# A conditioned feed-forward block: side 0 of the first pair turned by VectorE and transfers, output tiles, conditioning and weight sums in another order, a seed in an accumulator apart

## The chip, the core and the metric

The kernel runs on one NeuronCore of a Trainium2 chip. The metric is the device time of one execution in microseconds (us). The engines are TensorE (PE in the profile; its weight loads are PEld), VectorE (DVE), ScalarE (ACT), GpSimd (POOL) and SyncE (SP). SP computes nothing here: it issues transfers. Each engine runs its own queue strictly in the order in which the kernel writes it down, and waits for other engines by semaphores.

## The reference

Inputs are x of 32 sequences x 128 tokens x 512 channels, one condition vector of 512 per sequence, and a mask of the tokens (true only for the padding at the end of a sequence, so for few of them). In short:

```python
m = mask[:, :, None]
emb = silu(t) @ ada_w + ada_b                      # per sequence: shift, scale, gate
norm = where(m, layernorm(x) * (1 + scale) + shift, 0)
fwd = gelu(norm @ ssm_w1 + ssm_b1) @ ssm_w2 + ssm_b2      # bwd the same with its weights
x = x + gate_msa * where(m, fwd + bwd, 0)          # changes masked tokens only
shift_mlp, scale_mlp, gate_mlp = split(silu(t) @ ffada_w + ffada_b, 3)
ff_norm = layernorm(x) * (1 + scale_mlp) + shift_mlp
h = gelu_tanh(ff_norm @ ff_w1 + ff_b1)             # 512 -> 1024
out = x + gate_mlp * (h @ ff_w2 + ff_b2)           # 1024 -> 512
```

All is float32.

## The kernel before, in words

**Opening.** The first half changes masked tokens only, so the kernel collects them in 512 slots, four tiles of 128. For the first pair only slots 0 to 255 (tiles 0 and 1) matter. `hidden` (L184) makes the hidden layer of two tiles, `project` (L198) the second product into `po_s`, and `finish_slots` adds bias, multiplies by the gate, adds x (L200, L201, L289, on DVE) and stores the tile to `x1_rows` in DRAM (L290, SP). `take_first_half` (L652, POOL) then gathers the changed rows from there into the tiles of x; `Statistics` (L684 to L690; the root runs on POOL) and `normalised` (L696) make the normalised x.

Beside that the opening prepares the second half:

- `combine_weights` makes sums of the quarters of a weight matrix (four instructions of DVE), for `fw1` and later for `fw2`.
- `weight_sums(1)` to `weight_sums(4)` (L570, DVE) make further sums of `fw1` and store them to `t_rows` in DRAM (L572 to L575, SP), from where `load_weights` reads them as `tw`. Sums 1 and 4 use two tiles `spare` (named x), sums 2 the tile `t_2`, sums 3 a tile `tw_3` of its own.
- The conditioning of the second half: `pm_f` (L254, PE) is the product with `ffada_w`, `mod2` (L264, DVE) the result with its bias. It is transposed on PE into `ptr_mod` (L616) and copied to `modT`, from which the per-channel scale and shift come. Its gate rows go to `gate_rows` in DRAM (POOL).
- In the order of PE's queue: `po_s` of tile 0, `pm_f`, `po_s` of tile 1, the gate rows of tiles 2 and 3 (`part_s`, L274, which share three accumulators with `po_s` and `pm_f`), `ptr_mod`, then the hidden layer of tiles 2 and 3, and their `po_s`.

**The second half** takes the 32 sequences in four pairs of sides; a side is four sequences, so 512 tokens. Its input must lie with channels on the partitions (`xT`). In the first pair PE transposes the normalised tiles between the products of `po_s` (`transposed`, L705), and ACT (L714) and DVE (L710) in turn apply scale and shift. In the later pairs DVE turns blocks of 32 x 32 in place (STREAM_TRANSPOSE, L1225), 16 transfers per side put the blocks in place (`turned`, L725), and ACT scales them (`scaled`, L731).

`TokenBlocks` (L761, DVE) makes sums of the quarters of `xT` (s1, s2, a third that overwrites a quarter of side 1, and s4). The product with `ff_w1` is a scheme of seven products in place of eight, nested twice: seven products (numbers 1, 2, 5, 6, 3, 7, 4 in `STREAMS`), each made of seven phases P1 to P7. A phase (`FirstProduct.phase`, L879) is four passes on PE into one of two accumulators `e` and `a` of its product. P1, P6, P7 and P4 go to `a`, P5, P2 and P3 to `e`. After P5 `e` is copied away (`p_m`, L893); `seed` then puts `a` into `e` (L923 on DVE, L925 on ACT for product 1), and P2 adds to that. After P6 DVE writes `a` plus P5's result into `e` (L904), P3 adds to it; P7's and P4's results leave `a` through DVE (L909, L914). `window` interleaves the phases of a product with the last ones of the product before it, and puts smaller work, listed in `fills`, at places between them. `with_p5` (L930) and `late_sum` (L963) are sums on POOL.

The second product, with `fw2`, is one such scheme of 14 steps (`ORDER`, `SecondProduct.step`, L1059), into accumulators `a_o` and `e_o`; `first_block` (L1013) makes the sums that P5 takes. Between its first two steps stand the last phases of product 4, and `blocks(0, i)` for the next pair: normalise and turn sequence i of side 0.

The whole program is a `manual_schedule`: the order on each engine is that of the code.

Of the kernel before, what the change touches and what calls it, by code (L numbers as in the profile page):

```python
# [9 lines left out]
F32 = mybir.dt.float32  # L10
# [3 lines left out]
AF = mybir.ActivationFunctionType  # L14
# [8 lines left out]
def kernel(  # L23
# [49 lines left out]
    nc = tc.nc  # L73
# [217 lines left out]

    def combine_weights(w, rows, cols, t):

        b11, b12 = w[:, :rows, :cols], w[:, :rows, cols:]
        b21, b22 = w[:, rows:, :cols], w[:, rows:, cols:]
        t2, t3, t4 = (t[:, j] for j in range(3))
        nc.vector.tensor_tensor(t3, b22, b12, ALU.subtract)
        nc.vector.tensor_tensor(b12, b12, b11, ALU.subtract)
        nc.vector.tensor_tensor(t2, b22, b12, ALU.subtract)
        nc.vector.tensor_tensor(t4, b21, t2, ALU.subtract)  # L300
        return {"P1": b11, "P2": b21, "P3": b22, "P4": t4, "P5": b12, "P6": t2, "P7": t3}

# [242 lines left out]
    def in_blocks(t):  # L545
        return t.rearrange("p g (h f) -> p (g h) f", f=2 * P)
# [3 lines left out]
        2: [t_2.rearrange("p j k d -> p (j k) d")],  # L550
        4: [in_blocks(t) for t in spare],
    }

    def sum_block(j, n):
# [26 lines left out]
    for c in range(2):  # L581
        h1 += hidden(xT_s, NH, w1, 0, AF.Gelu, "s0", ssm, range(4 * c, 4 * c + 3))
        rows = slot_part(2 + c, 1, ps_o, "o"), slot_part(2 + c, 0, ps_o, "o")
        gs.append(keep_gate(c, slot_part(c, 2, ps_o, "o")))
        xn_s.append(modulated(xc[2 + c], *rows, f"s{2 + c}", xn[:, 2 + c]))
        if c == 0:
            combine_weights(fw1, KC // 2, FF // 2, t_1)
# [24 lines left out]
    gs = [keep_gate(c, slot_part(c, 2, ps_o, "o")) for c in (2, 3)]  # L612
# [87 lines left out]

    def transposed(g, xn, xT, k, by_vector):

        ptr = ps_t.tile([P, 512], F32, tag="tr", name=f"ptr_{g}_{k}")
        for i in range(G):
            nc.tensor.transpose(ptr[:, ts(i, P)], xn[i][:, ts(k, P)], ident)  # L705
        for i in range(G):
            b = g * G + i
            shift, scale = modT[:, k, b : b + 1], modT[:, k, B + b : B + b + 1]
            if by_vector:
                nc.vector.tensor_scalar(  # L710
                    xT[:, k, ts(i, P)], ptr[:, ts(i, P)], scale, shift, ALU.mult, ALU.add
                )
            else:
                nc.scalar.activation(  # L714
                    xT[:, k, ts(i, P)], ptr[:, ts(i, P)], AF.Identity, bias=shift, scale=scale
                )

# [81 lines left out]
    class FirstProduct:  # L799


        def __init__(self, p, x, w):
            self.p, self.x, self.w = p, x, w
            self.h = [
                hp.tile([P, HC, G * S], F32, tag=f"h{j}", name=f"h{j}_{p}") for j in "ab"
            ]
            self.banks, self.p5, self.tw = {}, {}, {}
            self.sx, self.held = {}, []

# [177 lines left out]
    class SecondProduct:  # L987
# [53 lines left out]
        def step(self, step):  # L1041
            p, ha, hb, s1, w = self.p, self.ha, self.hb, self.s1, fw2_of
            hh = HC // 2
# [72 lines left out]
    stats[1].one(0)  # L1116
    stats[1].one(1)

    def second_side():

        stats[1].one(2)
        stats[1].one(3)
        stats[1].root()
        for c in range(2):
            both = ssm.tile([P, 2, D], F32, tag="xT", name=f"xn_0_1_{c}", bufs=2)
            for i in range(2):
                xn_b.append(stats[1].normalised(2 * c + i, both[:, i]))

    xn_b = []

    def token_blocks(xT):
        of_x[0] = TokenBlocks(0, xT)
        for j in (1, 2, 3, 4):
            of_x[0].one(j)

    def turn(side, k):
        transposed(side, (xn_a, xn_b)[side], xT[side], k, by_vector=k % 2)

    def turns(*which):
        return lambda: [turn(side, k) for side, k in which]  # L1140

    finish_slots(
        2,
        h1,
        gs[0],
        {
            1: turns((0, 0)),
            2: turns((0, 1)),
            3: lambda: (second_side(), turn(0, 2)),
            4: turns((0, 3)),  # L1150
            6: turns((1, 0)),
            7: turns((1, 1)),
        },
    )
    finish_slots(3, h1, gs[1], {1: turns((1, 2)), 2: turns((1, 3)), 4: lambda: token_blocks(xT)})
    first_half.close()
# [15 lines left out]
    now.token_sums(2, 0)  # L1172
    now.do(1, "P7")
    now.with_p5(2, "22")
    now.token_sums(2, 1)
    now.do(2, "P2", "P6")
    now.token_sums(2, 2)
    now.token_sums(2, 3)
    now.do(1, "P4")
    for p in range(NP):  # L1180
        more_pairs = p + 1 < NP
# [24 lines left out]
        if more_pairs:  # L1206
            if p == 0:
                x_of[1] = load_x(1, spare)
            x_next = x_of[p + 1]
            stats = [Statistics(x_next[side], f"{p + 1}_{side}") for side in range(2)]  # L1210
            xn, xT = {}, {}

            def blocks(side, i):

                if i == 0:
                    t = (
                        group_of_tiles(f"{p + 1}_0")
                        if side == 0
                        else sp.tile([P, G, D], F32, tag="s12", name=f"xn_{p + 1}_1")
                    )  # L1220
                    xn[side] = t.rearrange("p i d -> p (i d)").rearrange(
                        "p (k i c) -> p k i c", i=G, c=P
                    )
                t = stats[side].normalised(i, xn[side][:, :, i])
                nc.vector.transpose(t, t)  # L1225
# [32 lines left out]
        fill = {5: [lambda: second.third_block(0)], 7: [lambda: second.third_block(1)]}  # L1258
        if more_pairs:

            def put(step, f, *args):
                fill.setdefault(step, []).append(lambda: f(*args))

# [159 lines left out]
```

## Time and profile before

| | before |
|---|---|
| median of 3 runs | 474.43 us (474.25 to 476.71) |
| the profiled execution | 474.88 us |
| its span, first to last instruction | 473.2 us |
| PE busy | 453.6 us, 96% |
| PEld busy | 367.9 us, 78% |
| DVE busy | 333.0 us, 70% |
| ACT busy | 175.5 us, 37% |
| POOL busy | 157.2 us, 33% |
| mean granted clock of PE | 0.996 |

Times in the profile count from the span's start. A line of a timeline has the start, the duration, the engine, the line of the kernel, the operation, the tiles written and read, the shape, and the number of instructions that are merged; in brackets the idle time of the engine ahead of it and what ended it. A line of the chain of waits has start, duration, what. A line of the windows view has the stretch, and for PE, PEld, DVE, ACT and POOL the busy time and number of instructions, then the granted clock, the share of the DMA engines that was busy, and GB/s. Rows of PE are overlapped: a pass of 256 columns is shown with 380 ns, but four in a row advance by 0.86 us.

### The profile page before, as it was taken

The page shows a single profiled execution, that of the slowest core. Times are in us where ns is not written, and L with a number is a line of the kernel's source. Part 1 is how long each engine was busy: PE and PEld are TensorE (multiplying, and loading weights), DVE is VectorE, ACT ScalarE, POOL GpSimd, SP SyncE. Part 2 cuts the span into 40 slices and gives each one's busy share as a digit, 9 for nine tenths or more (in the row PEclk, how much of TensorE's full clock was granted, in tenths as well). Part 3 has the DMA queues.
Part 4 walks back from the last instruction along what each step waited for, and adds up shares of the span by engine and source line. Part 5 has one row for each costly group of instructions (what it writes and reads, how often), then busy time and mean ns, then how long its engine had stood idle before and what let it go on. Part 6 is the DMA issues. An engine that isn't in the chain of part 4 may idle for free.

```text
span 473.2 us, 5833 instructions
## 1 busy us (share of the span) xinstructions
PE 453.6 (96%) x2016; PEld 367.9 (78%) x2016; DVE 333.0 (70%) x534; ACT 175.5 (37%) x380; POOL 157.2 (33%) x151
## 2 busy tenths in 40 slices
PE   6899997989999999999999999999999999999996
PEld 2374384458887888888878888888788888888885
DVE  4637686888778766997787488968875985433645
ACT  3122023325365074153643622545446134463000
POOL 6200035007975000189730002897200023760000
PEclk9999998999999999999999999999999999999999
DMA  8999930036314761844057428340773341303013
GB/s 277 386 408 355 403 151 14 23 130 242 110 57 118 150 89 46 320 166 160 3 175 125 100 75 280 129 159 3 215 104 82 123 167 33 124 34 145 0 61 120
DMA packets 73746, 69.35 MB, mean 147 GB/s; under 512 B 54689, under 2 KB 55217, under 8 KB 72691
## 3 DMA queue, kind: packets, MB, share of 16 engines
q1 hardware_dynamic: 63074, 57.42, 38.2%
q0 software_dynamic: 4256, 10.75, 6.7%
q10 hardware_dynamic: 6384, 0.79, 1.2%
q8 instruction: 17, 0.28, 0.2%
q14 instruction: 15, 0.11, 0.1%
HBM read 56.83 MB, written 13.17 MB: 148 GB/s over the span
## 4 chain that ended last, share of the span: by engine, by line
PE 56%; POOL 14%; DVE 11%; DMA 9%; issue 7%; ACT 1%; SPq 0%; POOLq 0%; DVEq 0%; ACTq 0%
PE a_o L1059 20%; PE e_o L1059 15%; PE a_m L879 9%; PE e_m L879 7%; POOL x L652 5%; DMA b2b<-in_L_cond_bwd_b_dram 4%; DVE xn L696 3%; POOL ha L930 2%; DMA t_rows<-x 2%; PE po_s L198 2%; DMA x<-x_rows,slot_i 2%; POOL ha L959 2%; POOL hb L959 2%; POOL hb L930 1%; DVE xn L1225 1%
## 5 line engine op out<-in xcount | busy, mean ns | idle before, releaser
L930 POOL TENSOR_TENSOR ha<-p_m,ha 128x512 f32<-128x512 f32 x20 | 27.7, 1387 | 172.8 <-ACT ha L937 163.6
L1059 PE MATMUL e_o<-fw,ha 128*128 128x256 f32 x256 | 57.9, 380 | 0.0
L1059 PE MATMUL a_o<-t,hb 128*128 128x256 f32 x240 | 54.1, 380 | 0.0
L1059 PEld LDWEIGHTS e_o<-fw,ha 128*128 128x128 f32 x256 | 48.8, 190 | 6.5
L1059 PEld LDWEIGHTS a_o<-t,hb 128*128 128x128 f32 x240 | 45.7, 190 | 6.1
L731 ACT ACTIVATE xT<-xT,modT 128x128 f32<-128x128 f32 x96 | 37.9, 479 | 25.9 <-DMA xT<-xn 25.8
L652 POOL DMA_INDIRECT x<-x_rows,slot_i x32 | 36.1, 1127 | 22.6 <-DMA x_rows<-t_s 13.9
L854 ACT ACTIVATE hb<-hb,biasT 128x256 f32<-128x256 f32 x64 | 29.0, 500 | 27.9 <-POOL hb L963 20.3
L893 ACT COPY p_m<-e_m 128x512 f32<-128x512 f32 x28 | 16.4, 586 | 60.1 <-PE e_m L879 60.1
L198 PE MATMUL po_s<-w,h_s 128*128 128x512 f32 x64 | 30.6, 614 | 0.0
L1059 PE MATMUL a_o<-t,s 128*128 128x256 f32 x128 | 28.9, 380 | 0.0
L1059 PE MATMUL a_o<-fw,ha 128*128 128x256 f32 x128 | 28.9, 380 | 0.0
L1059 PE MATMUL e_o<-fw,s 128*128 128x256 f32 x128 | 28.9, 380 | 0.0
L937 ACT COPY ha<-e_m 128x512 f32<-128x512 f32 x32 | 18.5, 579 | 27.7 <-PE e_m L879 23.8
L184 PE MATMUL ph_s<-xT_s,w 128*128 128x256 f32 x128 | 28.7, 383 | 0.0
L879 PE MATMUL a_m<-xT,tw 128*128 128x256 f32 x96 | 25.3, 386 | 3.5 <-DVE hb L909 3.5
L930 POOL TENSOR_TENSOR hb<-p_m,hb 128x512 f32<-128x512 f32 x20 | 28.2, 1411 | 0.3
L184 PEld LDWEIGHTS ph_s<-xT_s,w 128*128 128x128 f32 x128 | 24.0, 190 | 4.6 <-ACT h_s L188 1.5
L1059 PEld LDWEIGHTS a_o<-t,s 128*128 128x128 f32 x128 | 24.4, 190 | 3.2
L1059 PEld LDWEIGHTS a_o<-fw,ha 128*128 128x128 f32 x128 | 24.4, 190 | 3.2
L1059 PEld LDWEIGHTS e_o<-fw,s 128*128 128x128 f32 x128 | 24.4, 190 | 3.3
L684 DVE BATCH_NORM_STATS2 st<-x 128x6 f32<-128x512 f32 x32 | 21.9, 684 | 6.5 <-DMA x<-x_rows,slot_i 6.5
(194 smaller groups left out, 868.1 us busy)
## 6 DMA issues: line engine op xcount, KB each, us to landing
tw<-t_rows SPq DMA_DIRECT2D x16, 896.0 KB, 4.7
x<-in_x_dram SPq DMA_DIRECT2D x16, 512.0 KB, 6.9
gate<-gate_rows POOLq DMA_DIRECT2D x8, 1024.0 KB, 5.4
out_dram<-x SPq DMA_DIRECT2D x15, 512.0 KB, 3.3
xT<-xn SPq DMA_DIRECT2D x84, 64.0 KB, 2.8
fw<-in_L_cond_ff_w_dram SPq DMA_DIRECT2D x2, 2048.0 KB, 10.8
ada_f<-in_L_cond_ffada_w_dram SPq DMA_DIRECT2D x4, 768.0 KB, 16.0
ada_a<-in_L_cond_ada_w_dram SPq DMA_DIRECT2D x4, 512.0 KB, 6.2
```

Of the source, the lines that this page charges most:

```text
L184: nc.tensor.matmul(ph[:, :n], w[:, k, ts(f, P)], xT[:, k, :], start=(k == 0), stop=(k == KC - 1))
L198: nc.tensor.matmul(po, h[f][:, ts(i, P)], w[:, f, :], start=(f == 0), stop=(f == HC - 1))
L652: nc.gpsimd.indirect_dma_start(out=xs[i // G][i % G // 2][:, i % 2], out_offset=None, in_=x1_rows[:slots, :], in_offset=bass.IndirectOffse ...
L684: nc.vector.bn_stats(st, self.tile_at(i))
L731: nc.scalar.activation(xT[:, k, ts(i, P)], xT[:, k, ts(i, P)], AF.Identity, bias=modT[:, k, b : b + 1], scale=modT[:, k, B + b : B + b + 1],)
L854: nc.scalar.activation(dst[:, n], src[:, n], AF.Gelu_apprx_tanh, bias=biasT[:, f : f + 1])
L879: nc.tensor.matmul(bank[:, ts(n, QT)], self.w_block(j, product)[:, ts(n, P)], self.x_block(j, product), start=(product in ("P1", "P5") and ...
L893: nc.scalar.copy(p5, e)
L930: nc.gpsimd.tensor_tensor(self.place(RESULT[j], c), self.p5[j], other, ALU.add)
L937: nc.scalar.copy(self.place(RESULT[j], c), src)
L959: nc.gpsimd.tensor_tensor(part["12"], part["21"], other, ALU.add)
L1059: nc.tensor.matmul(part, src[:, k, ts(i, P)], w[product][:, k, :], start=(last and k == 0), stop=True, skip_group_check=True,)
```

## The change

1. `combine_weights` becomes a class, `Weights`, whose four sums can be made one at a time. For `fw2` they are no longer made together in the opening, but one each in windows 4 and 5 and in steps 2 and 6 of the second product of the first pair.
2. Weight sums 1 stand ahead of the sum of the biases; sums 3 and 4 directly behind slot tile 0, and slot tile 1 directly behind them. Sums 3 use the tiles of sums 1 again, sums 4 the tile `t_2` of sums 2. `mod2` comes after slot tile 1, on PE and on DVE. The store of `gate_rows` comes after the first six gathers.
3. Side 0 of the first pair is turned as in later pairs: by DVE and by 16 transfers, eight issued by SP and eight by ACT, then scaled on ACT. Side 1 is still transposed by PE, now only in slot tile 3 and behind it, and always scaled by DVE.
4. The first phases of products 1 and 2 come in another order, and product 1 has a third accumulator (`apart`): P5 goes into it, so that P1's result can be put into `e` before P5.
5. In every change of pair two of the four `blocks(0, i)` and the transfers come after phase P7 of product 4 instead of before P3, and the last statistic of side 1 comes later in window 6.

```diff
-    def combine_weights(w, rows, cols, t):
+    class Weights:
...
+            self.sums = [(t3, b22, b12), (b12, b12, b11), (t2, b22, b12), (t4, b21, t2)]
...
+        def combine(self, *which):
+            for j in which:
+                out, x, y = self.sums[j]
+                nc.vector.tensor_tensor(out, x, y, ALU.subtract)
...
         2: [t_2.rearrange("p j k d -> p (j k) d")],
-        4: [in_blocks(t) for t in spare],
     }
+    t_sum[3], t_sum[4] = t_sum[1], t_sum[2]
...
+    weight_sums(1)
     nc.vector.tensor_tensor(b2, b2, b2b, ALU.add)
     b2_row = dram.tile([1, D], F32, name="b2_row")
     nc.sync.dma_start(b2_row, b2[0:1, :])
-    weight_sums(1)
     weight_sums(2)
     finish_slots(0, h1, gs[0])
+    weight_sums(3)
+    weight_sums(4)
     transposed_slots(xn_s[1], xT_t[:, :, ts(1, P)], "s3")
+    finish_slots(1, h1, gs[1])
...
     modulation(pm, mod2, ada_f, modb_f, 0, 3)
-    gate_rows = dram.tile([B, D], F32, name="gate_rows")
-    nc.gpsimd.dma_start(gate_rows, mod2[2 * B : 3 * B, :])
...
-    t_sum[3] = [in_blocks(sp.tile([P, G, D], F32, tag="s12", name="tw_3"))]
-    weight_sums(3)
-    weight_sums(4)
-    finish_slots(1, h1, gs[1])
...
+        def apart(self, j):
+            e = ps_o.tile([P, 512], F32, tag="o", name=f"e_m{self.p}_{j}")
+            self.alone[j], a = accumulators(f"m{self.p}_{j}_alone")
+            self.banks[j] = e, a
+            self.p5[j] = None
...
             e, a = self.banks[j]
+            if product == "P5":
+                e = self.alone.pop(j, e)
...
     take_first_half(0, x_of[0], range(G + 2))
+    gate_rows = dram.tile([B, D], F32, name="gate_rows")
+    nc.gpsimd.dma_start(gate_rows, mod2[2 * B : 3 * B, :])
     h1 = hidden(xT_t, NH, w1, 0, AF.Gelu, "s1", ssm)
...
-    fw2_of = combine_weights(fw2, HC // 2, D // 2, t_2)
+    fw2_of = Weights(fw2, HC // 2, D // 2, t_2)
...
-    xn = group_of_tiles("0_0")
-    xn_a = [stats[0].normalised(i, xn[:, i]) for i in range(G)]
...
+    xn = in_turned_blocks(group_of_tiles("0_0"))
+    for i in range(G):
+        t = stats[0].normalised(i, xn[:, :, i])
+        nc.vector.transpose(t, t)
+    turned(xn, xT[0], (nc.sync, nc.scalar))
...
+    for k in range(KC):
+        scaled(0, xT[0], k)
...
-    finish_slots(3, h1, gs[1], {1: turns((1, 2)), 2: turns((1, 3)), 4: lambda: token_blocks(xT)})
+    finish_slots(2, h1, gs[0])
+    finish_slots(3, h1, gs[1], {4: lambda: turn(0), 6: lambda: turn(1)})
+    turn(2)
+    turn(3)
+    of_x[0] = TokenBlocks(0, xT)
+    for j in (1, 2, 3):
+        of_x[0].one(j)
...
+    now.apart(1)
     now.do(1, "P1")
+    now.seed(1)
     now.do(2, "P1")
+    now.do(1, "P2", "P5", "P6")
+    of_x[0].one(4)
+    now.do(2, "P5")
+    now.do(1, "P7")
+    now.with_p5(2, "22")
+    now.seed(2)
+    now.do(1, "P3")
+    now.with_p5(2, "12")
     for n in range(4):
         now.token_sums(1, n)
-    now.do(1, "P5")
-    now.seed(1)
-    now.do(2, "P5")
-    now.do(1, "P2", "P6", "P3")
-    now.seed(2)
-    now.with_p5(2, "12")
...
-    now.do(1, "P7")
-    now.with_p5(2, "22")
...
+                put(4, 1, fw2_of.combine, 0)
+                put(5, 1, fw2_of.combine, 1)
...
-            for i, at in enumerate(((4, 4), (4, 6), (5, 3), (6, 1))):
+            for i, at in enumerate(((4, 4), (4, 6), (5, 3), (6, 4))):
                 put(*at, stats[1].one, i)
...
         if more_pairs:
-            for i in range(G):
+            for i in range(2):
                 blocks(0, i)
-            to_feature_rows(0, nc.sync)
         now.do(4, "P3")
         second.seed(1)
         now.do(4, "P7")
+        if more_pairs:
+            for i in range(2, G):
+                blocks(0, i)
+            to_feature_rows(0, nc.sync)
         second.step(1)
...
+            put(2, fw2_of.combine, 2)
+            put(6, fw2_of.combine, 3)
```

More of the change, by code (lines that the diff above doesn't have):

```diff
@@ L290, in finish_slots, with __init__ @@
         nc.sync.dma_start(x1_rows[ts(at, P), :], t)
-    def combine_weights(w, rows, cols, t):
[L294 to L301, printed above, removed]
+    class Weights:
+        def __init__(self, w, rows, cols, t):
+            b11, b12 = w[:, :rows, :cols], w[:, :rows, cols:]
+            b21, b22 = w[:, rows:, :cols], w[:, rows:, cols:]
+            t2, t3, t4 = (t[:, j] for j in range(3))
+            self.sums = [(t3, b22, b12), (b12, b12, b11), (t2, b22, b12), (t4, b21, t2)]
+            self.of = {
+                "P1": b11, "P2": b21, "P3": b22, "P4": t4, "P5": b12, "P6": t2, "P7": t3
+            }
+        def combine(self, *which):
+            for j in which:
+                out, x, y = self.sums[j]
+                nc.vector.tensor_tensor(out, x, y, ALU.subtract)
     def x_tile(b):
@@ L586 @@
         if c == 0:
-            combine_weights(fw1, KC // 2, FF // 2, t_1)
+            Weights(fw1, KC // 2, FF // 2, t_1).combine(0, 1, 2, 3)
         h1 += hidden(xT_s, NH, w1, 0, AF.Gelu, "s0", ssm, range(4 * c + 3, 4 * c + 4))
@@ L699, in normalised, with transposed @@
             return t
-    def transposed(g, xn, xT, k, by_vector):
+    def transposed(g, xn, xT, k):
         ptr = ps_t.tile([P, 512], F32, tag="tr", name=f"ptr_{g}_{k}")
@@ L708, in transposed @@
             shift, scale = modT[:, k, b : b + 1], modT[:, k, B + b : B + b + 1]
[L709 to L716, printed above, removed]
+            nc.vector.tensor_scalar(
+                xT[:, k, ts(i, P)], ptr[:, ts(i, P)], scale, shift, ALU.mult, ALU.add
+            )
     def turned(xn, xT, queues):
@@ L807, in __init__ @@
             self.banks, self.p5, self.tw = {}, {}, {}
-            self.sx, self.held = {}, []
+            self.sx, self.held, self.alone = {}, [], {}
         def token_sums(self, j, n):
@@ L1041, in step @@
         def step(self, step):
-            p, ha, hb, s1, w = self.p, self.ha, self.hb, self.s1, fw2_of
+            p, ha, hb, s1, w = self.p, self.ha, self.hb, self.s1, fw2_of.of
             hh = HC // 2
@@ L1113, with in_turned_blocks, turn @@
     take_first_half(0, x_of[0], range(G + 2, 2 * G))
-    xn = group_of_tiles("0_0")
-    xn_a = [stats[0].normalised(i, xn[:, i]) for i in range(G)]
[L1116 to L1127, printed above, removed]
-    xn_b = []
[L1131 to L1154, printed above, removed]
-    finish_slots(3, h1, gs[1], {1: turns((1, 2)), 2: turns((1, 3)), 4: lambda: token_blocks(xT)})
+    def in_turned_blocks(t):
+        return t.rearrange("p i d -> p (i d)").rearrange("p (k i c) -> p k i c", i=G, c=P)
+    xn = in_turned_blocks(group_of_tiles("0_0"))
[3 more added lines that the diff above has]
+    turned(xn, xT[0], (nc.sync, nc.scalar))
+    for i in range(G):
+        stats[1].one(i)
+    stats[1].root()
+    xn_b = []
+    for c in range(2):
+        both = ssm.tile([P, 2, D], F32, tag="xT", name=f"xn_0_1_{c}", bufs=2)
+        for i in range(2):
+            xn_b.append(stats[1].normalised(2 * c + i, both[:, i]))
+    for k in range(KC):
+        scaled(0, xT[0], k)
+    def turn(k):
+        transposed(1, xn_b, xT[1], k)
+    finish_slots(2, h1, gs[0])
[5 more added lines that the diff above has]
+        of_x[0].one(j)
     first_half.close()
@@ L1161 @@
         now.load_weights(j)
+    now.apart(1)
     now.do(1, "P1")
+    now.seed(1)
     now.do(2, "P1")
+    now.do(1, "P2", "P5", "P6")
[6 more added lines that the diff above has]
+    now.with_p5(2, "12")
     for n in range(4):
         now.token_sums(1, n)
-    now.do(1, "P5")
-    now.seed(1)
-    now.do(2, "P5")
-    now.do(1, "P2", "P6", "P3")
-    now.seed(2)
-    now.with_p5(2, "12")
-    now.token_sums(2, 0)
-    now.do(1, "P7")
-    now.with_p5(2, "22")
-    now.token_sums(2, 1)
     now.do(2, "P2", "P6")
-    now.token_sums(2, 2)
-    now.token_sums(2, 3)
+    for n in range(2):
+        now.token_sums(2, n)
     now.do(1, "P4")
+    for n in range(2, 4):
+        now.token_sums(2, n)
     for p in range(NP):
@@ L1215, in blocks @@
                 if i == 0:
-                    t = (
+                    xn[side] = in_turned_blocks(
                         group_of_tiles(f"{p + 1}_0")
@@ L1219, in blocks @@
                         else sp.tile([P, G, D], F32, tag="s12", name=f"xn_{p + 1}_1")
-                    )
-                    xn[side] = t.rearrange("p i d -> p (i d)").rearrange(
-                        "p (k i c) -> p k i c", i=G, c=P
                     )
@@ L1246 @@
         if more_pairs:
-            for i in range(G):
+            for i in range(2):
                 blocks(0, i)
-            to_feature_rows(0, nc.sync)
         now.do(4, "P3")
@@ L1258, with put @@
         fill = {5: [lambda: second.third_block(0)], 7: [lambda: second.third_block(1)]}
+        def put(step, f, *args):
+            fill.setdefault(step, []).append(lambda: f(*args))
+        if p == 0:
+            put(2, fw2_of.combine, 2)
+            put(6, fw2_of.combine, 3)
         if more_pairs:
-            def put(step, f, *args):
-                fill.setdefault(step, []).append(lambda: f(*args))
             for i in range(G):
```

## The prediction

> **What bounds the kernel now.** I read the page's busy shares first, then TensorE's timeline, then the waits and the chain. TensorE (PE) is busy 96% of the span and ends 56% of the chain; the chain's other 44% lies almost all before 100 us.
>
> ```profile
> PE 453.6 (96%) x2016; PEld 367.9 (78%) x2016; DVE 333.0 (70%) x534; ACT 175.5 (37%) x380; POOL 157.2 (33%) x151
> ...
> PE 56%; POOL 14%; DVE 11%; DMA 9%; issue 7%; ACT 1%; SPq 0%; POOLq 0%; DVEq 0%; ACTq 0%
> ```
>
> So time is won or lost only where PE stands. Its timeline shows few such places: the opening between 74 and 106 us, and one wait of about 1 us at each of the three changes from one pair to the next.
>
> ```profile
> 76.78 1.76 PE L705 MATMUL ptr<-ident,xn 128*128 128x128 f32 x4 [2.70 <-DVE xn L696]
> ...
> 102.30 1.13 PE L879 MATMUL e_m<-xT,fw 128*128 128x256 f32 x4 [0.86 <-ACT e_m L925]
> ...
> 105.15 1.13 PE L879 MATMUL e_m<-s,fw 128*128 128x256 f32 x4 [0.86 <-DVE e_m L904]
> ...
> 150.28 1.13 PE L879 MATMUL a_m<-xT,tw 128*128 128x256 f32 x4 [1.14 <-DVE hb L909]
> ...
> 242.87 1.13 PE L879 MATMUL a_m<-xT,tw 128*128 128x256 f32 x4 [0.93 <-DVE hb L909]
> ```
>
> Ahead of that the chain of waits runs through memory: VectorE (DVE) waits for the store of the first weight sums, because it reuses their tiles; then it finishes slot tile 1, whose store releases the gathers.
>
> ```profile
> 46.14 10.87 DMA t_rows<-x
> ...
> 57.03 2.16 DVE x L570 x3
> ...
> 61.34 4.10 DMA x_rows<-t_s
> ```
>
> Meanwhile PE has work: 14 us of hidden layer from 59.15 us. It can start then because `mod2` was made early, ahead of the wait:
>
> ```profile
> 50.68 0.69 DVE L264 TENSOR_TENSOR mod<-pm_f,modb_f 96x512 f32<-96x512 f32 x1
> ...
> 57.03 1.29 DVE L570 TENSOR_TENSOR x<-fw,t 128x512 f32<-128x512 f32 x2 [3.47 <-DMA t_rows<-x]
> ```
>
> **What the Trainium skill says.** (1) "TensorE: Matmul & The Clock Gate", Part 1: a window of about 3.4 us without work halves PE's clock, and one busy window restores it. The trace agrees: after the standstill from 74 us the windows view shows the clock at 0.50 until about 81.5 us.
>
> ```profile
> 79.00:80.00 1.00, 1.00 (x2) 0.23 (x1) 0.59 (x2) 1.00 (x4) 0.00 (x0) 0.50 0.04 1
> ```
>
> (2) "DMA: Bandwidth & Descriptors", Queues, rings and completion order: each DMA engine takes descriptors in ring order. The trace agrees: the store issued at 46.14 lands 10.87 us later, behind the loads of fw2 and x, while the DMA share is 1.0. (3) The same page, Issuing engines are not separate DMA queues: a second issuing engine saves issue time only. (4) "ScalarE: Activation LUTs", What ACT_TABLE_LOAD costs: 280 ns + 0.833 ns per column, about 93 ns per further pointer operand; for 128 columns 480 ns. The trace has 479 (L731), and 37.9 us / 96 = 0.395 us apart in a row.
>
> **Part 1: weight sums 3 and 4 and slot tile 1 ahead of mod2.** Sums 1 no longer stand behind the bias `b2b`; they start at 41.1 instead of 43.8. But the x loads are issued until 45.62 on the same SP queue, so the store of sums 1 still leaves near 45.7 and lands near 57. Sums 3 now overwrite the tiles of sums 1, so DVE waits from 48.1 (slot tile 0 finished, 2 us earlier than now) to 57. Sums 4 overwrite `t_2` in place and wait for its store, 50.10 + 9.8 = 59.9 now; ring order keeps it there. So: sums 3 57.0-59.1, sums 4 59.9-62.0 (2.1 each, as now), slot tile 1 62.0-64.1 (2.2), `modb_f` and `mod2` (0.42 + 0.69) to 65.3. Queued behind these on DVE is `mod2`, and PE's queue has the transposes of `mod2` ahead of the hidden layer. PE itself moves `po_s1` up (7.1 us) and is through with `pm_f` and one gate row at 57.1, as now. Its second gate row needs the accumulator of slot tile 1 (62.7), then it stands until 65.3. The hidden layer starts near 66.0 instead of 59.15: **+6.8 us**. A standstill of 5.5 and then 2.3 us will nearly surely halve the clock; until a busy window has passed the loss is 0 to 3.4, and I take 2.0 (the shown case: 3.4 us at half speed, 1.7 lost). Hidden layer ends at 66 + 14 + 2 = 82 instead of 73.1.
>
> SP: the store of slot tile 1 leaves at 64.1, lands near 66.9 (now 65.4), and the gathers start 1.4 us later, at 67.6. On POOL `gate_rows` (0.63) now stands between the gathers and the root: root done at 78.2 instead of 76.05.
>
> **Part 2: side 0 by DVE and transfers.** Removed from PE: four groups of transposes at 0.44-0.60, about 2.2 us, and its waits for `xn` (2.70 and 0.50) with the half-clock window (1.7). Added on DVE: four STREAM_TRANSPOSE of 0.71, with the normalisation about 1.2 per tile (from 145.80 to 146.99): 78.2 to 83.1. Then 16 transfers of 64 KB, 8 on SP and 8 on ACT. The rows of 165-176 us show 0.65-0.72 to issue one and 3.1 to land; the program rotates eight semaphores over them, so that each waits for the landing of the eighth before it: 16 x 3.1 / 8 + 3.1 = 9.3, plus 0.9 as ACT first loads its table (1.28, until 84): last one at 93.3. Then 16 scalings on ACT, 0.395 each: done by 99.6, quarter by quarter. The weights' combination of fw2 (4 x 1.22) leaves DVE at 63-68 us, where it waits for gathers anyway: 0 here.
>
> PE after the hidden layer: slots 2 and 3 14.0, side 1's transposes 2.2: end at 97.9. DVE runs behind it: slot tile 3 (2.2) after 96.9, two groups from the transposes (2.7), then s1 at 103.0, s2 104.3.
>
> **Part 3: order of products, seed apart.** Both waits of 0.86 go. The two P1 run at 97.9-99.6. Product 1's seed now goes into another accumulator, but stands behind 16 scalings on ACT: P2 at 100.2 (wait 0.6). P5 needs s1: 103.1 (wait 2.0); P6 s2 (0.35); P3 the fourth block, which DVE makes after P6's sum (0.5); P2 of product 2 its seed (0.35). Eleven phases of 0.86 lead to the first phase of product 5 at **111.25, against 109.58 now: +1.7**. Without a halved clock it would be 109.3; add 0.3 for the chance that the wait of 2.0 triggers another half-clock window: **+2.0**. `e` banks: the third `o` accumulator is free at that point.
>
> **Part 4: combination of fw2 in windows and steps.** 4 x 1.22 us of DVE lie in windows 4 and 5 and second-product steps 2 and 6 of pair 0. DVE has gaps of 0.93 and 1.74 beside the first, little beside the second (it delays `hb` L909 to about 133.2, where PE wants its bank at 133.15); second-product slices show DVE 60-85% busy. **+0.2**; bounds 0 and 1.2 (one instruction fully exposed). If a cover went, the next product's `e_m` would be late.
>
> **Part 5: the three changes of pair.** Now four normalised and transposed tiles (4.8 us) stand ahead of `hb` L909, which frees the bank of P4. With two ahead, `hb` comes 2.4 us earlier than now, at 239.6 in pair 1, while PE wants it at 241.9: the wait goes. Moving the last statistic behind `hb` also removes the wait for a gather (0.23 and 0.26 on PE). Next in line is P5V, which needs `s1` (L1013) behind two GELUs; DVE's total ahead of it is unchanged, so it moves only with the removed gather wait (some 0.4) and needs ACT to follow: free at 246.5 for PE's 246.1-246.6, so just in time. Gain (1.14+0.19) + (0.93+0.23) + (0.91+0.26) = 3.66; I take 3.4, bounds 0.5 and 3.7. Side 0's transfers then start about when they do now.
>
> **Sum:** +2.0 + 0.2 - 3.4 = **-1.2 us**. The profiled execution took 474.88 (span 473.2, 1.7 around it), 0.45 above the median of 474.43; to the median: **473.2**. No change that can be told is about 0.5%, 2.4 us.
>
> **Rivals.** (a) *The opening's gap is smaller or absorbed* (the stores land before 57, or the clock stays up). For it: PE has later waits that swallow a delay. Against: the full DMA share until 62 us. With no gap at all the first normalised tiles of side 1 bind (88.3), product 5 starts at 107.3: -2.2 + 0.2 - 3.4 gives 469.0; with the gap at full clock 471.0. (b) *Slower: transfers of side 0 become the bound.* In the first change of pair they took from 149.75 until the scaling at 166.25, 16.5 us, on SP alone beside the gate's broadcast. At that price they land at 99.6, the seed comes at 106.7, PE stands 7 us and loses another 1.7: product 5 at about +7.0, total +3.8, 478.2. It costs from a landing after 95.2 and exceeds 0.5% from about 98. Against: two queues, no broadcast beside. (c) *The changes of pair do not pay*: P4's wait only moves to P5V; gain 0.5 gives 476.1. (d) *The seed apart does nothing*: it is part of the forecast, as the scalings stand ahead of it.
>
> **Chances.** Forecast 0.46 (own range 471.0 to 475.3), (a) 0.27, (b) 0.17, (c) 0.10. From (a) with the forecast's low end: faster 0.28; (b) with some of (c) and the forecast's high end: slower 0.24; the rest 0.48. Range for 8 in 10: 469.6 to 478.0, from (a) to (b).
>
> **What would show it.** Right: PE idle from 57 to 65 before L620 with the clock halved after; x DVE waits of some 9 us for t_rows; hidden layer ending near 82; transfers landing near 93; product 5 near 111; no PE wait on `hb` at the three changes. Wrong: `mod2` before 60, transfers beyond 95, or waits before P5V of about 1 us.

## The result, and the profile after

The changed kernel takes 479.51 us (median of 6 runs, 478.21 to 480.05), the kernel before 474.51 (6 runs, 473.89 to 476.71): a ratio of 1.0092, 95% interval 1.0067 to 1.0117. It is slower by 5.0 us, where 1.2 us faster was forecast. The profiled execution took 479.76 (span 478.0).

First the page, busy shares and the chain by engine:

```profile
PE 455.0 (95%) x2000; PEld 367.7 (77%) x2000; DVE 334.8 (70%) x538; ACT 175.4 (37%) x380; POOL 158.8 (33%) x151
...
PE 67%; POOL 5%; ACT 5%; DVE 5%; issue 3%; POOLq 0%; DVEq 0%; ACTq 0%
```

The sixteen transposes are gone, yet PE is busy 1.4 us longer: part of its work ran at half clock. PE carries more of the chain than before, since the opening's transfers and gathers have left it. What the shares don't tell, PE's timeline does (the places that answer to those shown of before):

```profile
62.18 2.07 PE L274 MATMUL part_s<-mod,pick 32*128 32x512 f32 x2 [4.93 <-DVE t_s L200]
...
65.96 16.67 PE L184 MATMUL ph_s<-xT_s,w 128*128 128x256 f32 x64
...
103.36 1.13 PE L891 MATMUL e_m_alone<-s,fw 128*128 128x256 f32 x4 [2.59 <-DVE s L760]
...
124.82 1.13 PE L891 MATMUL e_m<-xn_sy,tw 128*128 128x256 f32 x4 [2.29 <-DVE e_m L935]
125.79 1.86 PE L891 MATMUL a_m<-xn_sy,tw 128*128 128x256 f32 x4
127.44 1.91 PE L891 MATMUL a_m<-sx,tw 128*128 128x256 f32 x4
...
141.26 1.13 PE L891 MATMUL a_m<-xT,t 128*128 128x256 f32 x4 [0.67 <-DVE hb L921]
```

The waits for `xn`, the two of 0.86 and those for `hb` at the changes of pair are gone. The hidden layer starts at 65.96 as forecast. New is the wait of 2.29 at 124.82, and behind it two phases that last 1.65 and 1.71 from start to start, where one takes 0.86. The windows view (columns as before: the stretch, PE, PEld, DVE, ACT, POOL, then the granted clock) shows both half clocks, the opening's and this one:

```profile
64.00:67.00 3.00, 2.23 (x10) 1.60 (x10) 1.75 (x7) 0.58 (x1) 0.44 (x1) 0.50 0.45 169
...
126.00:128.00 2.00, 2.00 (x6) 1.55 (x6) 1.92 (x6) 0.58 (x1) 1.26 (x1) 0.50 0.00 0
```

DVE's timeline of the opening has the moved weight sums, `mod2` behind them, and the longer wait for the stores:

```profile
56.31 1.29 DVE L577 TENSOR_TENSOR x<-fw 128x512 f32<-128x512 f32 x2 [8.34 <-DMA t_rows<-x]
...
64.18 0.69 DVE L264 TENSOR_TENSOR mod<-pm_f,modb_f 96x512 f32<-96x512 f32 x1
```

Set against the profile before, four landmarks say where 4.8 us of span went:

| stretch of the span | before | after | difference |
|---|---|---|---|
| start to the first phase of product 5 | 109.58 | 111.88 | +2.3 |
| from there to step 0 of pair 0 (first `a_o`) | 30.76 | 36.40 | +5.6 |
| step 0 to step 2 in pairs 0, 1 and 2 | 10.91, 10.69, 10.68 | 9.50, 9.50, 9.50 | -3.8 |
| the rest | 300.6 | 301.2 | +0.6 |

The second line is the surprise: 0.2 was forecast for it. The waits of 2.29, 0.67 and 0.21 and the 1.64 lost at half clock make 4.8 of the 5.6. The seed `e_m` (L935) starts 12.2 us after product 5 instead of 8.6, and most of that is one instruction on DVE. DVE's timeline there, then POOL's:

```profile
119.20 0.68 DVE L830 TENSOR_TENSOR xT<-xT,xn_sy 128x512 f32<-128x512 f32 x1
...
121.00 2.83 DVE L830 TENSOR_TENSOR xT<-xT,xn_sy 128x512 f32<-128x512 f32 x1
123.75 0.41 DVE L830 TENSOR_TENSOR s<-s,xn_sy 128x256 f32<-128x256 f32 x1
124.08 0.68 DVE L935 TENSOR_TENSOR e_m<-a_m,ha 128x512 f32<-128x512 f32 x1
```

```profile
120.77 1.29 POOL L942 TENSOR_TENSOR ha<-p_m,ha 128x512 f32<-128x512 f32 x1
121.99 1.27 POOL L942 TENSOR_TENSOR hb<-p_m,hb 128x512 f32<-128x512 f32 x1
```

The same token sum takes 0.68 us at 119.20 and 2.83 at 121.00, and no wait is shown ahead of it. It ends 0.57 us, about its own length, after POOL's second sum. In the kernel before, the same sum was over when POOL's pair began; beside that pair DVE ran a statistic (one SBUF input) and `hb` (PSUM and SBUF) at full speed:

```profile
117.25 0.68 DVE L831 TENSOR_TENSOR xT<-xT,xn_sy 128x512 f32<-128x512 f32 x1
...
118.78 0.68 DVE L684 BATCH_NORM_STATS2 st<-x 128x6 f32<-128x512 f32 x1
...
119.60 0.66 DVE L909 TENSOR_TENSOR hb<-a_m,p_m 128x512 f32<-128x512 f32 x1
```

```profile
118.82 1.29 POOL L930 TENSOR_TENSOR ha<-p_m,ha 128x512 f32<-128x512 f32 x1
120.06 1.27 POOL L930 TENSOR_TENSOR hb<-p_m,hb 128x512 f32<-128x512 f32 x1
```

"SBUF — State Buffer" of the Trainium skill, section Who interferes with whom, says that a DVE instruction with two SBUF inputs contends with a GpSimd instruction that reads SBUF, and that one with at most one SBUF input does not. Both halves fit these lines. **Theory:** the two engines collide. **Rival:** that sum waits for data which the changed order brings late. The runs below tell the two apart, and size the parts.

### The profile page after: what moved, and what is told of

It reads as the page before. It is cut to its first block, busy times and chain, and to the rows that moved or that the text cites. A ratio compares the mean times of both kernels' runs of the same rounds, so it can differ in the third digit from the quotient of the medians.

```text
span 478.0 us, 5826 instructions
## 1 busy us (share of the span) xinstructions
PE 455.0 (95%) x2000; PEld 367.7 (77%) x2000; DVE 334.8 (70%) x538; ACT 175.4 (37%) x380; POOL 158.8 (33%) x151
## 4 chain that ended last, share of the span: by engine, by line
PE 67%; POOL 5%; ACT 5%; DVE 5%; issue 3%; POOLq 0%; DVEq 0%; ACTq 0%
PE a_o L1071 18%; PE e_o L1071 15%; PE a_m L891 14%; PE e_m L891 12%; PE ph_s L184 3%; PE po_s L198 3%; ACT hb L853 2%; POOL hb L975 2%; POOL ha L975 1%; POOL ha L942 1%; ACT ha L853 1%; POOL rstd L694 1%; PE last L1071 1%; DVE sx L820 1%; ACT a_o L1017 1%
## 5 line engine op out<-in xcount | busy, mean ns | idle before, releaser
L942 POOL TENSOR_TENSOR ha<-p_m,ha 128x512 f32<-128x512 f32 x20 | 27.2, 1362 | 153.0 <-ACT ha L949 143.5
L730 ACT ACTIVATE xT<-xT,modT 128x128 f32<-128x128 f32 x112 | 44.1, 480 | 34.6 <-DMA xT<-xn 34.6
L942 POOL TENSOR_TENSOR hb<-p_m,hb 128x512 f32<-128x512 f32 x20 | 29.7, 1487 | 23.7 <-DVE hb L921 23.3
L184 PE MATMUL ph_s<-xT_s,w 128*128 128x256 f32 x128 | 31.3, 406 | 0.0
L184 PEld LDWEIGHTS ph_s<-xT_s,w 128*128 128x128 f32 x128 | 25.8, 205 | 5.4 <-ACT h_s L188 1.5
L198 PE MATMUL po_s<-w,h_s 128*128 128x512 f32 x64 | 28.3, 593 | 0.0
L916 DVE TENSOR_TENSOR e_m<-a_m,ha 128x512 f32<-128x512 f32 x20 | 13.9, 697 | 16.6 <-POOL ha L942 6.6
L853 ACT ACTIVATE ha<-e_m,biasT 128x256 f32<-128x256 f32 x48 | 20.0, 468 | 14.9 <-PE e_m L891 9.9
```

The source lines that it names most:

```text
L184: nc.tensor.matmul(ph[:, :n], w[:, k, ts(f, P)], xT[:, k, :], start=(k == 0), stop=(k == KC - 1))
L198: nc.tensor.matmul(po, h[f][:, ts(i, P)], w[:, f, :], start=(f == 0), stop=(f == HC - 1))
L730: nc.scalar.activation(xT[:, k, ts(i, P)], xT[:, k, ts(i, P)], AF.Identity, bias=modT[:, k, b : b + 1], scale=modT[:, k, B + b : B + b + 1],)
L853: nc.scalar.activation(dst[:, n], src[:, n], AF.Gelu_apprx_tanh, bias=biasT[:, f : f + 1])
L916: nc.vector.tensor_tensor(e, a, p5, add)
L942: nc.gpsimd.tensor_tensor(self.place(RESULT[j], c), self.p5[j], other, ALU.add)
```

## The experiments

Each ratio is to the kernel before, run on the same chip beside it; that kernel's median was 474.8 to 475.1. The diffs are shortened to the lines that matter.

**Part 5 alone (before_blocks).** On the kernel before:

```diff
-for i, at in enumerate(((4, 4), (4, 6), (5, 3), (6, 1))):
+for i, at in enumerate(((4, 4), (4, 6), (5, 3), (6, 4))):
...
-for i in range(G): blocks(0, i)
-to_feature_rows(0, nc.sync)
+for i in range(2): blocks(0, i)
 now.do(4, "P3"); second.seed(1); now.do(4, "P7")
+for i in range(2, G): blocks(0, i)
+to_feature_rows(0, nc.sync)
```

> The kernel before with part 5 of the change alone: at each change of pair two of four normalised and turned tiles, and the transfers of side 0, come after P7 of product 4, and the last statistic of side 1 comes later. Theory: PE's waits on hb (L909; 1.14, 0.93 and 0.91 us, with 0.2 each before) go and nothing takes their place: 3.3 us less than before, about 471.2. Rival: the wait moves on to P5V, which needs s1: at most 0.5 less, about 474.0.

Measured: 472.30, ratio 0.9943 (0.9924 to 0.9962), a gain of 2.7. PE's waits for `hb` at the changes of pair are gone; in their place are two waits for `s1` of at most 0.2. Part 5 pays most of the 3.3 expected here, and rival (c) falls.

**Part 1 undone (after_sums_back).** On the changed kernel:

```diff
-weight_sums(3)
-weight_sums(4)
 transposed_slots(xn_s[1], xT_t[:, :, ts(1, P)], "s3")
-finish_slots(1, h1, gs[1])
...
+t_sum[3] = [in_blocks(sp.tile([P, G, D], F32, tag="s12", name="tw_3"))]
+weight_sums(3)
+weight_sums(4)
+finish_slots(1, h1, gs[1])
```

> The changed kernel with part 1 undone: sums 3 in a tile of their own, mod2 on PE and DVE ahead of sums 3, 4 and slot tile 1, gate_rows ahead of the gathers. Theory: the hidden layer starts near 59 at full clock and product 5 near 107.3 in place of 111.9, so at least 4.6 less: 474.9 if the stall of PE at 122.5 to 124.8 and its half clock stay, about 471 if they too go because DVE is ahead of POOL's sums again. Rival: the opening's delay is not what costs, since its later waits absorb it: about 479.

Measured: 475.07, ratio 0.9999 (0.9980 to 1.0017), 4.4 below the changed kernel. The hidden layer starts at 58.73 and takes 14.08, and product 5 starts at 107.63. Without that gap PE waits 2.1 at product 1's P2 for the seed on ACT, which stands behind the scalings. The stall of 2.29 stays, at 120.50, with its half clock: part 1 is not needed for it. (The edit also puts sums 1 behind the bias `b2b`, sums 4 into `spare` and `gate_rows` behind `mod2`, as before.)

**Two token sums moved (after_late_sums4).** On the changed kernel, pair 0 alone:

```diff
-((2, 4), (2, 4), (2, 6), (2, 6))     # places of the four token sums 4
+((2, 4), (2, 4), (3, 3), (3, 3))
```

> The changed kernel, with the last two token sums of number 4 (pair 0) moved from the end of window 2 to after P7 in window 3. Theory: the third of these sums took 2.83 us in place of 0.68 because it reads two SBUF tiles while POOL runs two sums (L942) back to back; moved away from there, PE's wait of 2.29 us and the half clock behind it (about 1.7) go: 3.9 less than the changed kernel, about 475.6, and these sums take 0.7 each. Rival 1: it is slow wherever it stands, so the wait moves with it: about 479.5. Rival 2: DVE is simply 2 us behind all along, so the next seed is as late: about 479.

Measured: 477.21, ratio 1.0049 (1.0032 to 1.0066). The stall and its half clock are gone; product 5 to step 0 takes 33.56 instead of 36.40. Of the gain 2.3 us is left in the medians. In this profile the clock is halved in the opening instead, from about 103.7 to 107.2, behind the wait of 2.59 for `s`:

```profile
104.00:107.00 3.00, 3.00 (x9) 2.37 (x8) 2.04 (x3) 0.00 (x0) 0.00 (x0) 0.50 1.02 403
```

In the changed kernel's profile the same wait has no half clock behind it, so of the two losses only the stall is clearly saved. The run moves DVE's order, though, so a rival that speaks of late data is not excluded.

**Part 4 undone (after_combine_back).** On the changed kernel:

```diff
 fw2_of = Weights(fw2, HC // 2, D // 2, t_2)
+fw2_of.combine(0, 1, 2, 3)
...
-put(4, 1, fw2_of.combine, 0)
-put(5, 1, fw2_of.combine, 1)
...
-put(2, fw2_of.combine, 2)
-put(6, fw2_of.combine, 3)
```

> The changed kernel with part 4 undone: the four sums of fw2 stand together in the opening again. Theory: they cost only where the second of them (2.33 us at 138.3) holds back hb, which PE waits 0.67 us for: 0.7 to 1.0 less than the changed kernel, about 478.7. Rival: the four sums load DVE so that it falls behind in windows 3 to 5 altogether: 3 less, about 476.5.

Measured: 479.45, ratio 1.0100 (1.0077 to 1.0123): no change, where 0.7 to 1.0 less was expected. The wait for `hb` is gone (0.67 to none), a wait of 0.5 for the seed on ACT is new, and the stall of 2.29 stays. Its profiled execution took 477.5, 2 below its own median. It kept its clock after the stall, but not in the opening: there it is halved from about 103.6 to 107.1, behind the wait for `s`.

**POOL's sums later (after_pool_later).** The test of the collision from POOL's side; DVE and PE keep their order:

```diff
-put(2, 6, take_first_half, p + 1, x_next, range(G, G + 2))
-put(3, 4, take_first_half, p + 1, x_next, range(G + 2, G + 3))
+put(2, 6, take_first_half, p + 1, x_next, range(G, G + (3 if p == 0 else 2)))
+if p:
+    put(3, 4, take_first_half, p + 1, x_next, range(G + 2, G + 3))
```

> The changed kernel with one of pair 1's gathers (slot tile G+2) moved on POOL from window 3 to window 2 of pair 0, so that POOL's two sums L942 of product 6 start one gather (1.3 us) later; DVE's order and PE's order are untouched. Theory (DVE and POOL collide in SBUF): the third L830 sum, at 121.0, takes 0.68 instead of 2.83, the seed e_m (L935) comes near 121.9 instead of 124.08, PE's wait of 2.29 at 124.82 and the half clock after it go; the gain is 2.3 (as when the sums were moved) to 3.9 us, so 475.6 to 477.2. Rival (the third L830 waits for data, or DVE is simply behind on its line): the sum stays at 2.8 us and the wait at 2.3, the time at 479.5.

Its DVE timeline, then POOL's:

```profile
121.92 0.67 DVE L830 TENSOR_TENSOR xT<-xT,xn_sy 128x512 f32<-128x512 f32 x1
122.51 0.41 DVE L830 TENSOR_TENSOR s<-s,xn_sy 128x256 f32<-128x256 f32 x1
122.85 0.68 DVE L935 TENSOR_TENSOR e_m<-a_m,ha 128x512 f32<-128x512 f32 x1
```

```profile
121.98 1.49 POOL L656 DMA_INDIRECT x<-x_rows,slot_i  x1 [0.30 <-issue]
123.49 1.28 POOL L942 TENSOR_TENSOR ha<-p_m,ha 128x512 f32<-128x512 f32 x1
```

With nothing on DVE changed the sum takes 0.67, beside a gather that POOL issues, and the seed comes at 122.85. PE's wait of 2.29 and the half clock are gone. The rival falls. The time, 478.33, ratio 1.0077 (1.0050 to 1.0103), misses its expectation: 1.2 lower than the changed kernel, with intervals that overlap. The stretch from product 5 to step 0 is again 33.56 (-2.8), but this execution reached product 5 at 112.80, behind a half clock from about 104.5 to 107.9. The same edit on a kernel with part 1 undone (below) gives a clear difference.

**POOL's sums earlier (before_pool_early).** On the kernel before, one gather of pair 1 from (2, 6) to (3, 4):

```diff
-put(2, 6, take_first_half, p + 1, x_next, range(G, G + 2))
+put(2, 6, take_first_half, p + 1, x_next, range(G, G + (1 if p == 0 else 2)))
```

> The kernel before with one of pair 1's gathers (slot tile G+1) moved on POOL from window 2 to window 3 of pair 0, so that POOL's two sums L930 of product 6 start at about 117.5 instead of 118.82; nothing else is moved. Theory (collision): the third or the fourth L831 sum (at 117.25 and 117.84, 0.68 and 0.42) lasts until POOL's pair is over, at 120.1 to 120.5; the seed e_m (L923) comes about 2 us later than 118.18, the e_m phase at 119.07 waits some 1.8 us, and the time is 476.5 if the clock stays and 478.5 if a half clock follows. Rival (the collision is not the cause): nothing is stretched, 474.5.

Measured: 474.79, ratio 0.9998 (0.9983 to 1.0012). The run decides nothing: in its profiled execution DVE was 1.5 us earlier too, through with these sums at 116.79, and POOL's pair started at 117.35. There was no collision to see.

**A collision made on the kernel before (before_late_sums).**

```diff
-((2, 4), (2, 4), (2, 6), (2, 6))     # places of the four token sums 4, pair 0
+((2, 4), (2, 4), (3, 2), (3, 2))
```

> The kernel before with the last two token sums 4 of pair 0 (L831) moved two phases later, behind the seed and the first statistic, so that DVE comes to them at about 118.7 where POOL starts its two sums L930 (118.82 to 121.33). In the profile of before_pool_early the collision did not come about, since DVE was through with these sums before POOL's pair; this run makes it on the kernel before from DVE's side. Collision: the first of the two, or the second if the first slips in ahead, lasts until POOL's pair is over (1.5 to 2.8 us in place of 0.68 or 0.42), hb (L909, 119.6) and e_m (L904, 121.81) come about 2 us later, PE waits 1 to 2 us for e_m or hb near 123 to 126, and the time is 475.5 to 478. Rival (only the changed kernel has something that slows this sum): both take 0.68 and 0.42 and the time is 475.0.

Its timelines of DVE, POOL and PE:

```profile
116.42 0.66 DVE L831 TENSOR_TENSOR xT<-xT,xn_sy 128x512 f32<-128x512 f32 x1
117.00 4.13 DVE L831 TENSOR_TENSOR s<-s,xn_sy 128x256 f32<-128x256 f32 x1
121.05 0.68 DVE L909 TENSOR_TENSOR hb<-a_m,p_m 128x512 f32<-128x512 f32 x1
```

```profile
117.13 1.28 POOL L930 TENSOR_TENSOR ha<-p_m,ha 128x512 f32<-128x512 f32 x1
118.36 1.26 POOL L930 TENSOR_TENSOR hb<-p_m,hb 128x512 f32<-128x512 f32 x1
119.58 1.26 POOL L959 TENSOR_TENSOR ha<-ha 128x512 f32<-128x512 f32 x1
```

```profile
121.78 1.50 PE L879 MATMUL a_m<-sx,tw 128*128 128x256 f32 x4 [3.44 <-DVE hb L909]
```

Measured: 478.56, ratio 1.0088 (1.0057 to 1.0119), so +3.7, a little more than expected. Three sums of POOL stood in a row, and behind PE's wait the clock was halved from about 122.4 to 125.8. A sum of half the size (0.42 elsewhere) took 4.13 us and ended 0.29 after the third. Two instructions moved by two phases cost the kernel before nearly as much as the whole change did. The collision needs nothing of the changed kernel.

**Part 1 alone (before_sums).** On the kernel before:

```diff
+weight_sums(1)
 nc.vector.tensor_tensor(b2, b2, b2b, ALU.add)
...
 finish_slots(0, h1, gs[0])
+weight_sums(3)
+weight_sums(4)
 transposed_slots(xn_s[1], xT_t[:, :, ts(1, P)], "s3")
+finish_slots(1, h1, gs[1])
...
 pm = ps_o.tile([P, 512], F32, tag="o", name="pm_f")
...
-weight_sums(3)
-weight_sums(4)
-finish_slots(1, h1, gs[1])
```

(Its tiles for sums 3 and 4 and the place of `gate_rows` are also those of the changed kernel.)

> The kernel before with part 1 alone (weight sums 3 and 4 and slot tile 1 ahead of mod2). The hidden layer starts near 66 instead of 59.15 and ends near 82.5 instead of 73.06, a delay of 9.4. If part 1's cost passes through as it did in the changed kernel: PE's later waits for xn (2.70, 0.50) and their half clock (1.7) swallow 4.9 of it, product 5 starts at about 114.1 instead of 109.58, and the time is 479. Rival (the opening is bound by the chain through DVE and the gathers, and the later hidden layer is nearly free): 474.5 to 476.

Measured: 480.10, ratio 1.0100 (1.0069 to 1.0131), +5.0 and 1.1 above the expectation. The hidden layer runs 65.63 to 81.99, product 5 starts at 113.08. The rival, an opening bound by gathers, falls: PE's later wait for `xn` shrinks to 0.56, but the two waits of 0.86 stay, and most of the delay passes through.

**Parts 1 and 4 undone, POOL's sums later (after_best).** The diffs of after_sums_back, after_combine_back and after_pool_later together, on the changed kernel.

> The changed kernel with part 1 undone, part 4 undone (fw2 combined in the opening) and POOL's two sums of product 6 one gather later, as a version that may beat both. If the costs add as the single runs showed: 475.07 (part 1 undone) - 2.3 to 3.9 (stall) - 0 to 0.7 (hb wait) = 470.5 to 472.8, with product 5 at 107.6 and step 0 of pair 0 at 138 to 139 (before: 140.34). If the collision only moves to another DVE sum: 475.

Measured: 470.64, ratio 0.9922 (0.9897 to 0.9948): faster than both kernels. In its timeline of PE the changes of pair and the stretch ahead of them are nearly clean; no wait behind product 5's start is above 0.21:

```profile
118.68 1.13 PE L894 MATMUL e_m<-xn_sy,tw 128*128 128x256 f32 x4
...
139.62 3.62 PE L1074 MATMUL a_o<-fw,ha 128*128 128x256 f32 x16
```

**The same with part 4 left in (after_sums_back_pool).** The diffs of after_sums_back and after_pool_later.

> after_best with part 4 as in the changed kernel (fw2 combined in windows 4 and 5 and steps 2 and 6). It tells what part 4 is worth once the stall is gone: if the L308 instruction beside POOL's L942 sums makes hb late as in the changed kernel (0.67 to 0.85 us on PE), the time is 0.7 to 1.0 above after_best, 471.4; if POOL hides it or the opening gains what the windows lose (DVE is 4.9 us freer at 63 to 68 us), 470.6 as after_best.

Measured: 471.58, ratio 0.9925 (0.9900 to 0.9949). Against after_best the medians differ by 0.9, the ratios by 0.0003: what part 4 costs lies between nothing and 0.9, and `hb` is late by 0.84 on PE again. Against after_sums_back, from which it differs by POOL's one gather alone, it gains 3.5 us (0.9999 to 0.9925, intervals apart). That is the price of the collision with what hangs on it, and the test on the time that after_pool_later did not give. In the profiles a half clock is part of it: after_sums_back has one behind the stall, from about 121.3 to 124.7, and this kernel has none there.

**Parts 2 and 3 alone (turned_alone).** after_best with the diff of before_blocks taken back.

> after_best with part 5 undone too: parts 2 and 3 alone (side 0 turned by DVE and transfers, the other order with the seed apart), with POOL's sums one gather later. If the parts add: before 475.0 less 1.6 to 2.0 (product 5 at about 107.9 in place of 109.58), so 473.1; PE again waits about 1 us for hb at each change of pair. If parts 2 and 3 are only worth something with the new pair changes behind them, or only move the wait on: 475.

Measured: 473.88, ratio 0.9975 (0.9961 to 0.9988): -1.0, half of the expectation, and the wait of 1.09 for `hb` is back at the change of pair. Turning side 0 on DVE and the other order are worth a little, if POOL's sums keep out of the way.

## Why the prediction was wrong

By its own steps:

| step | forecast | measured |
|---|---|---|
| hidden layer of tiles 2 and 3 starts | 66.0 | 65.96 |
| lost there at half clock | 2.0 | 2.6 (16.67 - 14.08) |
| transfers of side 0 landed | 93.3 | 91.7, then 16 scalings in 6.26 |
| wait for the seed behind the scalings | 0.6 | none |
| P5 on s1 | wait 2.0, to 103.1 | 2.59, to 103.36 |
| product 5 in the profile | 111.25 | 111.88 |
| product 5 to step 0 (part 4) | +0.2 | +5.6 |
| three changes of pair (part 5) | -3.4 | -3.8 in the profile, -2.7 in the medians |

**Two steps failed.** The first is "Part 4 ... **+0.2**; bounds 0 and 1.2", the only term for the stretch from product 5 to step 0. Profiles of four cases, each of one or two executions, show what it left out. The stretch takes 31.66 with neither the collision nor part 4 (after_best), 33.49 with part 4 alone (after_sums_back_pool), 33.86 with the collision alone (after_combine_back, at full clock there), and 36.34 and 36.40 with both and a half clock (after_sums_back and the changed kernel). So in this stretch the collision and part 4 cost about 2 us each. Part 4's share is a collision too: its second sum, priced at 1.22, came beside POOL's pair, took 2.33 and held back `hb`:

```profile
138.28 2.33 DVE L308 TENSOR_TENSOR fw<-fw 128x1024 f32<-128x1024 f32 x1
```

```profile
138.26 1.27 POOL L942 TENSOR_TENSOR ha<-p_m,ha 128x512 f32<-128x512 f32 x1
139.48 2.25 POOL L942 TENSOR_TENSOR hb<-p_m,hb 128x512 f32<-128x512 f32 x1
```

In the medians, which hold the opening as well, part 4 costs only 0 to 0.9.

The stall of 2.29 comes from the order, not from part 4. It is absent with part 1 or part 5 alone, stays when part 1 or part 4 is undone, and part 5 lies later in time; so by elimination it comes with parts 2 and 3, which were run alone only with POOL's gather moved. It costs 3.5 us in one pair of kernels, 2.3 and 1.2 in two others, 2.8 in the profiles.

The prediction priced POOL's and DVE's instructions each by the mean of its row and asked only which waits for which. It compared no two of them that run at the same time, though two instructions with no semaphore between them can stop each other. The profile before had the sign: in each of the three later pairs one L828 sum takes 1.75 where it takes 0.71 in the first pair, beside a sum of POOL, and PE doesn't wait for it:

```profile
201.50 1.75 DVE L828 TENSOR_TENSOR s<-s 128x512 f32<-128x512 f32 x1
```

```profile
201.26 1.44 POOL L930 TENSOR_TENSOR hb<-p_m,hb 128x512 f32<-128x512 f32 x1
```

How parts 2 and 3 bring it about was read in the traces, not tried. Product 2's two sums L942 on POOL (108.76 to 111.70) lie beside the token sums `sx`, which take 1.53 and 2.36 (two) where the kernel before had 0.69 and 1.29 with POOL idle. DVE is some 1.9 us later from there, and reaches the third L830 sum 9.1 us after product 5's start instead of 7.7, when POOL's second pair has begun (8.9; 9.2 before).

The second is the size of the opening's term, "111.25, against 109.58 now". That 111.25 met 111.88 is in part luck: in the three other profiled kernels with this opening product 5 starts at 112.19 to 112.80, and there the wait for `s` was followed by a half clock, for which the prediction had put 0.3 as a chance. And 109.58 was taken from one execution. In the three other profiled kernels with the opening before it comes at 108.40, 108.07 and 106.95, with waits for `xn` of 1.30 to 1.92 where the quoted one had 2.70, and in one of them no half clock. "Removed from PE" therefore counted as a gain what is partly an accident of one run. Four profiles of the opening before average 108.3, four of the opening after 112.3: +4.0 and not +2.0. In the medians part 1 costs 4.4 (taken out) or 5.0 (put in), and parts 2 and 3 give 1.0.

An early product 5 is not kept in the kernel before, though. Step 0 comes at 140.34 in its profile, at 140.16 in before_blocks and at 140.09 in before_pool_early: the two that start early wait 1.00 and 1.03 for `e_m` (L904) at 129, which DVE makes only behind POOL's sum `ha` (L959). So the first two lines of the table of landmarks hold as a sum, 7.9, and less so one by one.

So the medians add up as part 1 +4.4 to 5.0, parts 2 and 3 -1.0, collision +1.2 to 3.5, part 4 0 to 0.9, part 5 -2.7: between +1.9 and +5.7, with the measured +5.0 inside. The lower end and the large scatter of the collision say that the parts do not simply add.

**Of the rivals,** (a) is refuted: the gap is neither smaller nor absorbed. (b), the one on the slow side, had the wrong mechanism: transfers landed at 91.7, and it needed 95.2. (c) is refuted by before_blocks. For (d), both waits of 0.86 are gone, but where part 1 is undone PE waits 1.9 to 2.9 for the seed, as ACT comes to it behind the scalings; no run takes the third accumulator alone away. Nor does a run issue the transfers of side 0 from one engine, so what the second engine saves is not shown. No rival named POOL beside DVE; the range reached to 478.0, and the result is 1.5 beyond it.

## What to carry to other kernels

Before moving an instruction of DVE with two SBUF operands, lay DVE's and POOL's timelines on top of each other: a sum that runs into POOL's sums can last to the end of their run (2.8 and 4.1 us here), not its own 0.4 to 0.7 us, and PE loses time where it waits for that sum. A row whose duration is several times that of its twins, with no wait in brackets, is the sign. And take a landmark that waits and half clocks precede from several executions before counting its gaps as gain.

## What the runs showed of the hardware that was not expected

- **The block can outlast one instruction, and mostly does not.** "SBUF — State Buffer" of the Trainium skill, SBUF: two separate sides, calls the shared ports an exclusive lock that is held for the whole instruction, while the other engine blocks. Mostly DVE got in after one instruction of POOL: in the changed kernel `sx` (1.53 at 109.04) and the L308 sum (2.33 at 138.28) each ran between POOL's two sums, the second of which then took 1.71 and 2.25 instead of 1.27. But the L830 sum was held over both of POOL's sums (2.83, in three kernels alike), and the L831 sum of before_late_sums over three (4.13). What decides between the two was not found.
- **The length of one wait alone does not tell whether the clock is halved.** The wait of 2.29 for L935 was followed by a half clock in the changed kernel and in after_sums_back, and by none in after_combine_back. The wait of 2.59 for `s` was followed by one in after_late_sums4 and after_pool_later, and by none in the changed kernel. In openings with the clock full until then, a wait of 1.30 was followed by one (before_blocks), and waits of 1.92 (before_late_sums) and 2.87 (turned_alone) were not. All these waits are shorter than the 3.4 us without work that the prediction quotes. What agrees is how long a half clock lasts: 3.4 us each time behind such a wait, and 10.2 us, from 61.0 to 71.2, in the changed kernel's opening, where it begins within the wait of 4.93. What else decides was not tried.
